# An LSTM layer on one core: a product of its own for f*c, other queues for some loads and stores, and more buffers

## Chip, cores and metric

The kernel runs on one core of a Trainium2 chip. The metric is the device time in microseconds (us) of one execution. The profile comes from one execution, recorded by the hardware profiler.

## What is computed

An LSTM over T=512 steps for a batch of 32, with D=H=512, all in fp32, whose input is added to its output. Cut to what matters:

```python
xW = einsum('ntd,dg->ntg', x, Wx) + b          # all steps at once
c = zeros
for t in range(512):
    a = xW[:, t] + h @ Wh                      # 32 x 2048
    i, f, o = sigmoid(a[:, :512]), sigmoid(a[:, 512:1024]), sigmoid(a[:, 1024:1536])
    g = tanh(a[:, 1536:])
    c = f * c + i * g
    h = o * tanh(c)
    y[:, t] = h
out = y + x
```

Only h @ Wh and the cell depend on the step before. The rest, xW, can be computed ahead.

## The kernel before, in words

**The recurrent part.** A state tile holds 128 partitions (4 blocks j of 32 batch rows, each for a quarter of the units) by 4 gates x 128 units. `h_part(t)` is 32 matmuls on PE, each 128x32 weights of h against a 128x512 slice of Wh (line L203), into one of two PSUM banks (`gbank`). That bank already holds the step's xW, put there by ACT (`seed_step`, L581). `cell(t)` then runs on ACT and VectorE (DVE): ACT does the sigmoid of i and f in one go (L217), tanh of g (L218), sigmoid of o (L219). VectorE makes i*g and f*c in one product of 128x256 (`prod`, L220), since c is kept beside g in the state tile `s`; then two adds of 64 units each (L222); ACT takes tanh of c in two halves (L224); VectorE multiplies by o (L226) and transposes (L232) into `ht`, which the next h_part needs. POOL adds x to it (L237), and SP stores two steps at a time (L241).

**The fill.** While the cell runs, PE computes xW for later steps. For 480 of the 512 steps it uses a fast matrix product in the manner of Strassen: steps are taken in 20 groups of 24. Each group has 20 slots; a slot has 7 products of sums of x by sums of Wx. The sums of x (U, `ubuf`) are made on VectorE (L381); the sums of weights are made once, at the start (L621), and stored in DRAM (`vdram`, six DMAs for a slot, L635); from there a ring of three SBUF rows, `vring`, is loaded in a fixed order (L544), one row of 896 KB for 7 products. The products (L470) go to `xbank` and `bbank`; ACT and VectorE move them to `cbuf` (L516, L522, L525, L526, L529, L532), VectorE sums them into results (L346), and SP stores results in DRAM (`xwd`, L362). Three steps ahead of its use, SP loads a step's xW from there into `xw` (`load_xw`, L568: four DMAs of 32 rows, 64 KB each). In a step, 46 or 48 matmuls of this fill ("passes", 128x256 each) stand behind h_part on PE.

**The head.** The first 24 steps' xW is made by plain products with the whole of Wx, in four chunks a step ("plain blocks", L164). The first five are made before step 0; after that most steps up to t=9 carry two plain blocks each. `keep` (L701) adds the bias to a finished block in one of two parks, which lie in `cbuf`, and SP stores it to `kept` in DRAM (L702). VectorE makes the weight sums meanwhile, and SP issues their stores (`flush_v`) after the next h_part. The stream of fast products begins at t=10. ACT's queue issues the loads of the bias (L709) and of two bias seeds (L676) at the very start; SP issues x, Wx, h0 and Wh.

**The tail.** The last 8 steps' xW is again plain, and the stream is over at about t=475. For this Wx is loaded once more (16 DMAs at t=477). From t=482 (`SPLIT`) each step is done in two halves: h_part in two halves of columns (64 matmuls), and a cell for each half, so that one half's cell runs beside the other half's matmuls. The two steps before SPLIT carry three plain chunks each, later ones carry one.

**What sets the order.** The instructions of each engine run in the order in which the program issues them (a manual schedule). In a step that is: h_part; on SP the stores of weight sums, of outputs and of kept blocks, the results' stores, the loads of x and xW; evacuation, seeds, vring loads, VectorE's sums as far as a planner's budget of time (`room`) reaches; the fill; the cell. Hardware DMAs issued by SP and by ACT share eight semaphores ("lanes") in turn, so a DMA is issued only when the one eight before it has landed.

Of the kernel before, what the change touches and what calls it, by code (L numbers as in the profile page):

```python
# [33 lines left out]
SPLIT = 482  # L34
# [54 lines left out]
def kernel(  # L89
# [22 lines left out]
    NC = 10  # L112
# [14 lines left out]
    h_init = const.tile([P, NJ, B], F32, name="h_init")  # L127
# [17 lines left out]
    late_weights = [False]  # L145

    def raw(blk):

        if late_weights[0] and blk < 6:
            return xs0[:, blk].rearrange("p s m -> p (s m)").rearrange("p (s c) -> p s c", s=4)  # L150
        return r1[:, blk]
# [16 lines left out]
    state = {"ht": h_init}  # L168
    sring = [work.tile([P, 2, 4, H], F32, name=f"s_{i}") for i in range(2)]
    oring = [work.tile([P, 2, H], F32, name=f"o_{i}") for i in range(1)]  # L170
    prod = work.tile([P, 2, 2, H], F32, name="prod")
    tanh_c = work.tile([P, P], F32, name="tanh_c")
    hbuf = work.tile([P, P], F32, name="hbuf")
    htr = [work.tile([P, NJ, B], F32, name=f"ht_{i}") for i in range(3)]
    ocr = [work.tile([P, 2, NJ, B], F32, name=f"oc_{i}") for i in range(2)]
    x_last = work.tile([P, P], F32, name="x_last")
# [30 lines left out]
    def cell(t):  # L207
# [3 lines left out]
        ht = htr[t % 3]  # L211
        by_gate = lambda a: a.rearrange("p (h g u) -> p h g u", g=G, u=H)
        for part in [(0,), (1,)] if is_split(t) else [(0, 1)]:
# [6 lines left out]
            nc.vector.tensor_mul(prod[:, i], s[:, i, 0:2], s[:, i, 2:4])  # L220
            for u in part:
                add(nxt[:, u, 3], prod[:, u, 0], prod[:, u, 1])  # L222
# [336 lines left out]
    def load_xw(t):  # L559
# [7 lines left out]
        for j in range(NJ):  # L567
            nc.sync.dma_start(  # L568
                out=dst[j * B : (j + 1) * B], in_=xwd[g % 2][m, q * B : (q + 1) * B, j]
            )  # L570
# [61 lines left out]
    def v_store(s, parts):  # L632
        lo, hi = parts
        to = lambda k: vdram[(s + k) % R]
        dma = lambda o, i: nc.sync.dma_start(out=o, in_=i)  # L635
        dma(to(0)[:, 0:2], lo[:, 0:2])
        dma(to(0)[:, 3], hi[:, 0])
        dma(to(1)[:, 2], lo[:, 2])
        dma(to(1)[:, 4], hi[:, 1])
# [9 lines left out]
    def v_slot(s):  # L649
# [4 lines left out]
        if len(terms) > 1:  # L654
            d = v_add(terms)
            v_stores.append(lambda: v_store(s, (vroom[d][:, 0:3], vroom[d][:, 3:7])))
            free_v.append(d)
        else:
            (i,) = terms
            parts = v_parts(i)  # L660
            v_stores.append(lambda: v_store(s, parts))
# [32 lines left out]
    parks = [cbuf[:, 8, 2 * i : 2 * i + 2].rearrange("p s c -> p (s c)") for i in range(2)]  # L694
# [3 lines left out]
    def keep(p):  # L698
        n = p - KEPT
        dst = parks[n % 2]  # L700
# [3 lines left out]
    with tc.manual_schedule():  # L704
# [3 lines left out]
        for j in range(NJ):  # L708
            nc.scalar.dma_start(  # L709
                out=bias_full[j * B : (j + 1) * B], in_=bias[j : j + 1].to_broadcast([B, W])  # L710
            )
        load_seeds(((4, 3), (5, 1)), nc.scalar)
        load_x(0, 0, 5)
        for c in range(4):
# [3 lines left out]
                in_=wx[c].rearrange("p (j c) -> p j c", j=NJ),  # L718
            )
# [7 lines left out]
        load_x(2)  # L727
        load_group(0)
# [28 lines left out]
        late_seeds_due = [late_seeds]  # L757
        s_done = {0: 4}
# [6 lines left out]
        for t in range(T):  # L765
# [17 lines left out]
            if t < HEAD_STEPS:  # L783
# [15 lines left out]
                for i, (kind, m) in enumerate(chunks):  # L799
                    if kind == "plain":  # L800
# [4 lines left out]
                        if i == 0:  # L805
                            cell(t)
# [7 lines left out]
                    else:  # L814
# [13 lines left out]
                        if i == 0:  # L828
                            cell(t)
# [107 lines left out]
```

## Time and profile before

| what | us |
| --- | --- |
| median of three runs | 3230.72 (3230.59 to 3233.8) |
| the profiled execution | 3234.63 |
| its span in the profile | 3232.8 |
| PE busy | 3163.2 (98% of the span) |
| VectorE busy | 2112.2 (65%) |
| ACT busy | 1342.8 (42%) |
| POOL busy | 233.9 (7%) |

The granted TensorE clock of the profiled execution was 0.992 of full speed in the mean. DMA engines moved 766.63 MB, 237 GB/s over the span.

By stages of the span (us), busy time of the engines, clock and DMA share:

| stretch | PE busy | VectorE busy | ACT busy | PE clock | DMA share |
| --- | --- | --- | --- | --- | --- |
| 60 to 80 | 19.01 | 8.70 | 1.85 | 1.00 | 0.69 |
| 80 to 100 | 12.41 | 8.69 | 1.61 | 0.91 | 0.79 |
| 100 to 120 | 8.78 | 10.70 | 1.61 | 0.74 | 0.62 |
| 120 to 140 | 16.25 | 11.62 | 2.49 | 0.91 | 0.78 |
| 140 to 160 | 18.59 | 10.01 | 3.21 | 1.00 | 0.49 |
| 160 to 180 | 10.20 | 4.17 | 2.52 | 0.74 | 0.75 |
| 180 to 200 | 18.64 | 12.46 | 7.42 | 1.00 | 0.73 |
| 200 to 240 | 38.37 | 31.22 | 17.84 | 1.00 | 0.81 |
| 240 to 280 | 34.35 | 28.00 | 14.66 | 0.96 | 0.69 |
| 400 to 3040 | 2638.35 | 1798.12 | 1154.19 | 1.00 | 0.77 |
| 3040 to 3100 | 48.13 | 23.62 | 16.73 | 0.91 | 0.61 |
| 3100 to 3200 | 100.00 | 45.29 | 47.75 | 1.00 | 0.24 |
| 3200 to 3232 | 25.95 | 15.43 | 13.47 | 0.99 | 0.06 |

How to read it: "busy" counts an engine's computing instructions, not the issue of DMAs. Matmuls are pipelined and their ends are modelled, so a PE that is busy for a whole stretch need not be at its peak. A wait is written as engine, tile and line of the waiting instruction, then "<-" and what released it, then the total in us, the number of times and the longest. In a timeline the bracket holds the idle time before the instruction and its releaser.

### The profile page before, as it was taken

Reading aid. Unit: us, or ns where it says so; the run is one execution under the profiler, and the core shown is the slowest. Engines: PE = TensorE matmul, PEld = TensorE weight load, DVE = VectorE, ACT = ScalarE, POOL = GpSimd, SP = SyncE. Lnnn points to the kernel's source line nnn. Section 1 sums busy time; section 2 is a strip of 40 time slices with the busy share of each in tenths; the row PEclk is TensorE's granted clock in tenths of the full one; section 3 lists DMA queues with packets and bytes.
Section 4 is the critical chain, followed back from the end, with each engine's and each line's share of the span. In section 5 each row is a group of like instructions: output and inputs, shape, how many; then the busy total and the mean of one; then the engine's idle time right before and its main releaser. Section 6 shows DMA issues by size and latency. Waiting matters only on the chain.

```text
span 3232.8 us, 102212 instructions
## 1 busy us (share of the span) xinstructions
PE 3163.2 (98%) x41304; PEld 1582.9 (49%) x41304; DVE 2112.2 (65%) x5721; ACT 1342.8 (42%) x4509; POOL 233.9 (7%) x508
## 2 busy tenths in 40 slices
PE   9789999999999999999999999999999999999999
PEld 4344545444444544444444544454444444444455
DVE  3566667676766667676666667676766767676634
ACT  0133444444444444444444444444444444444344
POOL 0000000000000000000000000000000000000000
PEclk9899999999999999999999999999999999999999
DMA  6677787877778777777777777877777777777641
GB/s 248 223 270 256 225 269 223 262 241 247 244 250 258 230 253 233 256 240 253 240 259 251 239 255 228 260 239 252 236 258 251 246 247 235 251 250 232 211 125 40
DMA packets 307080, 766.63 MB, mean 237 GB/s; under 512 B 49840, under 2 KB 95920, under 8 KB 306096
## 3 DMA queue, kind: packets, MB, share of 16 engines
q1 hardware_dynamic: 306128, 759.30, 73.1%
q8 instruction: 326, 5.34, 0.7%
q14 instruction: 146, 1.20, 0.1%
q10 hardware_dynamic: 480, 0.79, 0.1%
HBM read 577.18 MB, written 182.71 MB: 235 GB/s over the span
## 4 chain that ended last, share of the span: by engine, by line
PE 90%; DVE 1%; ACT 1%; issue 0%; DMA 0%; ACTq 0%; DVEq 0%
PE gbank L203 52%; PE xbank L470 31%; PE bbank L470 5%; PE xbank L203 2%; PE xbank L164 1%; DVE prod L220 0%; ACT s L217 0%; ACT tanh_c L224 0%; DVE ht L232 0%; DVE s L222 0%; DVE hbuf L226 0%; DMA xwd<-cbuf 0%; DVE cbuf L346 0%; ACT s L218 0%; DVE ubuf L381 0%
## 5 line engine op out<-in xcount | busy, mean ns | idle before, releaser
L203 PE MATMUL gbank<-wh_sb,ht 128*32 128x512 f32 (+1 forms) x16256 | 1809.1, 584 | 38.9 <-DVE ht L232 31.6
L470 PE MATMUL xbank<-vring,ubuf 128*32 128x256 f32 x14400 | 1110.6, 379 | 11.6 <-DMA vring<-vdram 9.8
L203 PEld LDWEIGHTS gbank<-wh_sb,ht 128*32 128x32 f32 x16256 | 577.8, 110 | 991.1 <-issue 755.9
L470 PEld LDWEIGHTS xbank<-vring,ubuf 128*32 128x32 f32 x14400 | 649.1, 110 | 378.7 <-issue 182.1
L220 DVE TENSOR_TENSOR prod<-s 128x256 f32<-128x256 f32 (+1 forms) x542 | 221.2, 408 | 853.6 <-ACT s L218 852.1
L217 ACT ACTIVATE s<-gbank 128x256 f32<-128x256 f32 (+1 forms) x509 | 192.1, 377 | 1376.8 <-PE gbank L203 1358.6
L346 DVE TENSOR_TENSOR cbuf<-cbuf 128x1024 f32<-128x1024 f32 x480 | 577.3, 1217 | 2.1
L237 POOL TENSOR_TENSOR oc<-xnat,ht 128x128 f32<-128x128 f32 x504 | 233.7, 464 | 2961.2 <-DVE ht L232 1478.9
L224 ACT ACTIVATE tanh_c<-s 128x64 f32<-128x64 f32 x1024 | 209.8, 249 | 387.5 <-DVE s L222 386.6
L581 ACT COPY gbank<-xw 128x512 f32<-128x512 f32 x477 | 285.0, 597 | 4.2 <-DMA xw<-xwd 4.0
L226 DVE TENSOR_TENSOR hbuf<-o,tanh_c 128x64 f32<-128x64 f32 x1024 | 192.8, 225 | 137.1 <-ACT tanh_c L224 137.0
L470 PE MATMUL bbank<-vring,ubuf 128*32 128x256 f32 x2400 | 277.0, 380 | 0.6 <-DVE cbuf L522 0.6
L516 ACT COPY cbuf<-xbank 128x512 f32<-128x512 f32 x400 | 231.6, 579 | 42.1 <-PE xbank L470 35.7
L470 PE MATMUL xbank<-vring,r 128*32 128x256 f32 x2400 | 239.0, 379 | 0.0
L470 PE MATMUL xbank<-vring,xs 128*32 128x256 f32 x2400 | 234.2, 381 | 1.0 <-ACT xbank L500 1.0
L222 DVE TENSOR_TENSOR s<-prod 128x64 f32<-128x64 f32 x1024 | 187.5, 222 | 18.6
L232 DVE STREAM_TRANSPOSE ht<-hbuf 128x64 f32<-128x64 f32 x1022 | 194.0, 225 | 6.6 <-DVE ht L232 0.4
L522 DVE TENSOR_TENSOR cbuf<-bbank,cbuf 128x256 f32<-128x256 f32 x400 | 162.9, 407 | 15.0 <-issue 12.6
L529 DVE TENSOR_TENSOR cbuf<-xbank,cbuf 128x256 f32<-128x256 f32 x400 | 161.9, 405 | 0.6 <-PE xbank L470 0.4
L526 DVE TENSOR_TENSOR cbuf<-xbank,cbuf 128x256 f32<-128x256 f32 x400 | 160.8, 402 | 1.7 <-ACT cbuf L525 1.7
L532 ACT COPY cbuf<-xbank 128x256 f32<-128x256 f32 x400 | 147.7, 369 | 19.8 <-PE xbank L470 3.1
L470 PEld LDWEIGHTS xbank<-vring,r 128*32 128x32 f32 x2400 | 122.8, 110 | 64.8 <-issue 38.1
(85 smaller groups left out, 1676.6 us busy)
## 6 DMA issues: line engine op xcount, KB each, us to landing
vring<-vdram SPq DMA_DIRECT2D x397, 896.0 KB, 6.3
xwd<-cbuf SPq DMA_DIRECT2D x240, 512.0 KB, 7.0
xw<-xwd SPq DMA_DIRECT2D x1920, 64.0 KB, 4.4
out_dram<-oc SPq DMA_DIRECT2D x255, 128.0 KB, 2.9
xnat<-in_x_dram SPq DMA_DIRECT2D x63, 512.0 KB, 5.0
xs<-in_x_grouped_dram SPq DMA_DIRECT2D x10, 1536.0 KB, 10.1
r<-in_x_grouped_dram SPq DMA_DIRECT2D x10, 1536.0 KB, 10.0
vdram<-vring SPq DMA_DIRECT2D x40, 128.0 KB, 1.9
```

The lines of the kernel that those rows point to most:

```text
L203: nc.tensor.matmul(dst[j * B : (j + 1) * B], state["ht"][:, k], m, start=False, stop=True, skip_group_check=True)
L217: nc.scalar.activation(s[:, i, 0:2], g[:, :, 0:2], AF.Sigmoid)
L220: nc.vector.tensor_mul(prod[:, i], s[:, i, 0:2], s[:, i, 2:4])
L222: add(nxt[:, u, 3], prod[:, u, 0], prod[:, u, 1])
L224: nc.scalar.activation(tanh_c[:, HALVES[u]], nxt[:, u, 3], AF.Tanh)
L226: nc.vector.tensor_mul(hbuf[:, HALVES[u]], o[:, u], tanh_c[:, HALVES[u]])
L232: nc.vector.transpose(ht[:, 2 * u : 2 * u + 2].rearrange("p q b -> p (q b)"), hbuf[:, HALVES[u]])
L237: (nc.gpsimd if t < T - 8 else nc.vector).tensor_add(oc[:, tt % 2], x_of(t), ht)
L346: op(c_of(dst), c_of(src), c_of(bb))
L470: nc.tensor.matmul(dst[q * B : (q + 1) * B], left_of(gr, s, r)[:, q * B : (q + 1) * B], vring[:, row % 3, RIGHT[r]], start=start, stop=Tru ...
L516: nc.scalar.copy(t[:, 0:4:3], xb.rearrange("p (n c) -> p n c", n=2))
L581: nc.scalar.copy(bank_of(t), src)
```

## The change

Six edits come together:

- **The cell.** `prod` is replaced by `fc` (f*c, 128x128, both halves at once) and `ig` (i*g, two products of 64 units). fc stands first, then the two i*g, then the two adds.
- **Stores of weight sums.** They are issued by ACT's queue in place of SP's, after the first cell of a step instead of after h_part; where a sum lies whole in one tile (14 of 20 slots), two of the six DMAs become one. The loads of the bias and of the early seeds go from ACT's queue to SP's, behind Wx and behind x; the late seeds are loaded by ACT's queue, one step after the last plain block, and made later.
- **Buffers.** Four parks instead of two, eleven `cbuf` buffers instead of ten; two `ht` buffers instead of three, and `h_init` and `x_last` lie in other buffers.
- **xW loads.** One DMA for a step, whose source pattern has the four blocks j as its outermost dimension, instead of four DMAs.
- **vring.** Its first rows may be loaded as soon as five or fewer jobs of VectorE are left and all stores of weight sums are issued, rather than at the first stream step.
- **Tail.** Wx is reloaded by six DMAs, one in each step from t=469; SPLIT is 478 instead of 482; the two steps before it carry two plain chunks instead of three.

```diff
@@ -31,7 +31,7 @@
 KEPT = 5
 AHEAD = 28
 STREAM0 = HEAD + GS - AHEAD
-SPLIT = 482
+SPLIT = 478
 U_SUMS = {6: {3: 1, 5: -1}, 7: {1: 1, 6: 1}, 8: {2: 1, 3: -1}, 9: {2: 1, 7: -1}, 10: {0: 1, 1: -1}, 11: {0: 1, 4: -1}}
 U_OF = [
@@ -109,7 +109,7 @@
     bbank = psum.tile([P, W], F32, name="bbank")
     gbank = [psum.tile([P, W], F32, name=f"gbank_{i}") for i in range(2)]
-    NC = 10
+    NC = 11
     r1 = const.tile([P, 8, 4, HW], F32, name="r1")
     cbuf = const.tile([P, NC, 4, HW], F32, name="cbuf")
     r2 = cbuf[:, 0:8]
@@ -124,7 +124,6 @@
     seeds = [r1[:, 6 + i // 2, i % 2 * 2 : i % 2 * 2 + 2].rearrange("p s c -> p (s c)") for i in range(4)]
     seeds += [seeds_own[:, i] for i in range(2)]
     bias_full = const.tile([P, W], F32, name="bias_full")
-    h_init = const.tile([P, NJ, B], F32, name="h_init")
     xw = const.tile([P, 3, W], F32, name="xw")
     vdram = dram.tile([R, P, 7, HW], F32, name="vdram")
@@ -143,12 +142,11 @@
         return xnat[:, xslot(t // TC), t % TC]
     late_weights = [False]
+    late_r = xs0.rearrange("p k s m -> p k (s m)").rearrange("p k (s c) -> p k s c", s=4)
     def raw(blk):
-        if late_weights[0] and blk < 6:
-            return xs0[:, blk].rearrange("p s m -> p (s m)").rearrange("p (s c) -> p s c", s=4)
-        return r1[:, blk]
+        return (late_r if late_weights[0] and blk < 6 else r1)[:, blk]
     def plain_block(t, c, bank):
@@ -165,15 +163,28 @@
                     d, x_of(t)[:, c], m, start=c == 0 and n == 0, stop=True, skip_group_check=True
                 )
-    state = {"ht": h_init}
+    def late_load(c, a, b):
+        rows = wx[c].rearrange("p (j s c) -> p j s c", j=NJ, s=2)
+        dst = late_r if a < 6 else r1
+        return lambda: nc.sync.dma_start(
+            out=dst[:, a:b, c % 2 * 2 : c % 2 * 2 + 2], in_=rows[:, a % 4 : a % 4 + b - a]
+        )
+
+    late_loads = [late_load(0, 0, 4), late_load(1, 0, 4), late_load(2, 4, 6), late_load(3, 4, 6)]
+    late_loads += [late_load(2, 6, 8), late_load(3, 6, 8)]
+
+    state = {}
     sring = [work.tile([P, 2, 4, H], F32, name=f"s_{i}") for i in range(2)]
     oring = [work.tile([P, 2, H], F32, name=f"o_{i}") for i in range(1)]
-    prod = work.tile([P, 2, 2, H], F32, name="prod")
+    fc = work.tile([P, 2, H], F32, name="fc")
+    ig = work.tile([P, 2, H], F32, name="ig")
     tanh_c = work.tile([P, P], F32, name="tanh_c")
     hbuf = work.tile([P, P], F32, name="hbuf")
-    htr = [work.tile([P, NJ, B], F32, name=f"ht_{i}") for i in range(3)]
+    htr = [work.tile([P, NJ, B], F32, name=f"ht_{i}") for i in range(2)]
     ocr = [work.tile([P, 2, NJ, B], F32, name=f"oc_{i}") for i in range(2)]
-    x_last = work.tile([P, P], F32, name="x_last")
+    x_last = vring[:, 0, 0, 0:P]
+    h_init = htr[1]
+    state["ht"] = h_init
     HALVES = [slice(0, H), slice(H, P)]
     PAIRS = [[xbank[0], xbank[1]], [gbank[0], gbank[1]]]
@@ -208,7 +219,7 @@
         n, tt = divmod(t, TC)
         s, nxt = sring[t % 2], sring[(t + 1) % 2]
         o = oring[0]
-        ht = htr[t % 3]
+        ht = htr[t % 2]
         by_gate = lambda a: a.rearrange("p (h g u) -> p h g u", g=G, u=H)
         for part in [(0,), (1,)] if is_split(t) else [(0, 1)]:
             i = slice(part[0], part[-1] + 1)
@@ -217,9 +228,11 @@
             nc.scalar.activation(s[:, i, 0:2], g[:, :, 0:2], AF.Sigmoid)
             nc.scalar.activation(s[:, i, 2], g[:, :, 3], AF.Tanh)
             nc.scalar.activation(o[:, i], g[:, :, 2], AF.Sigmoid)
-            nc.vector.tensor_mul(prod[:, i], s[:, i, 0:2], s[:, i, 2:4])
+            nc.vector.tensor_mul(fc[:, i], s[:, i, 1], s[:, i, 3])
             for u in part:
-                add(nxt[:, u, 3], prod[:, u, 0], prod[:, u, 1])
+                nc.vector.tensor_mul(ig[:, u], s[:, u, 0], s[:, u, 2])
+            for u in part:
+                add(nxt[:, u, 3], fc[:, u], ig[:, u])
             for u in part:
                 nc.scalar.activation(tanh_c[:, HALVES[u]], nxt[:, u, 3], AF.Tanh)
             for u in part:
@@ -564,10 +577,7 @@
         g, n = divmod(t - HEAD, GS)
         assert getattr(group(g), "stored", 0) >= 4 * (n // 8 + 1), (t, group(g).__dict__.get("stored"))
         m, q = divmod(n, 4)
-        for j in range(NJ):
-            nc.sync.dma_start(
-                out=dst[j * B : (j + 1) * B], in_=xwd[g % 2][m, q * B : (q + 1) * B, j]
-            )
+        nc.sync.dma_start(out=dst, in_=xwd[g % 2][m, q * B : (q + 1) * B].rearrange("b j c -> j b c"))
     xw_late = {}
@@ -629,14 +639,17 @@
             if v_uses[i] == 0:
                 free_v.append(vt[i])
-    def v_store(s, parts):
+    def v_store(s, parts, whole=None):
         lo, hi = parts
         to = lambda k: vdram[(s + k) % R]
-        dma = lambda o, i: nc.sync.dma_start(out=o, in_=i)
+        dma = lambda o, i: nc.scalar.dma_start(out=o, in_=i)
         dma(to(0)[:, 0:2], lo[:, 0:2])
         dma(to(0)[:, 3], hi[:, 0])
-        dma(to(1)[:, 2], lo[:, 2])
-        dma(to(1)[:, 4], hi[:, 1])
+        if whole is None:
+            dma(to(1)[:, 2], lo[:, 2])
+            dma(to(1)[:, 4], hi[:, 1])
+        else:
+            dma(to(1)[:, 2:5:2], whole[:, 2:5:2])
         dma(to(2)[:, 5], hi[:, 2])
         dma(to(3)[:, 6], hi[:, 3])
@@ -653,12 +666,12 @@
             v_sum(i)
         if len(terms) > 1:
             d = v_add(terms)
-            v_stores.append(lambda: v_store(s, (vroom[d][:, 0:3], vroom[d][:, 3:7])))
+            v_stores.append(lambda: v_store(s, (vroom[d][:, 0:3], vroom[d][:, 3:7]), vroom[d]))
             free_v.append(d)
         else:
             (i,) = terms
             parts = v_parts(i)
-            v_stores.append(lambda: v_store(s, parts))
+            v_stores.append(lambda: v_store(s, parts, vroom[vt[i]] if i > 7 else None))
             v_used(i)
     v_stores = []
@@ -691,13 +704,13 @@
-    parks = [cbuf[:, 8, 2 * i : 2 * i + 2].rearrange("p s c -> p (s c)") for i in range(2)]
+    parks = [cbuf[:, 8 + i // 2, i % 2 * 2 : i % 2 * 2 + 2].rearrange("p s c -> p (s c)") for i in range(4)]
     park_banks = [xbank[1], xbank[2], bbank]
     kept_stores = []
     def keep(p):
         n = p - KEPT
-        dst = parks[n % 2]
+        dst = parks[n % 4]
         add(dst, park_banks[n % 3], bias_full)
         kept_stores.append(lambda: nc.sync.dma_start(out=kept[n], in_=dst))
@@ -705,17 +718,16 @@
         nc.vector.memset(sring[0], 0.0)
         nc.vector.memset(tanh_c, 0.0)
         nc.scalar.activation(hbuf, tanh_c, AF.Sigmoid)
-        for j in range(NJ):
-            nc.scalar.dma_start(
-                out=bias_full[j * B : (j + 1) * B], in_=bias[j : j + 1].to_broadcast([B, W])
-            )
-        load_seeds(((4, 3), (5, 1)), nc.scalar)
         load_x(0, 0, 5)
         for c in range(4):
             ko, ki = divmod(c, 2)
             nc.sync.dma_start(
                 out=r1[:, 4 * ko : 4 * ko + 4, 2 * ki : 2 * ki + 2].rearrange("p j s c -> p j (s c)"),
                 in_=wx[c].rearrange("p (j c) -> p j c", j=NJ),
+            )
+        for j in range(NJ):
+            nc.sync.dma_start(
+                out=bias_full[j * B : (j + 1) * B], in_=bias[j : j + 1].to_broadcast([B, W])
             )
         nc.sync.dma_start(out=h_init.rearrange("p q b -> p (q b)"), in_=h0)
         for k in range(NJ):
@@ -725,6 +737,7 @@
         load_x(0, 5, 8)
         load_x(1)
         load_x(2)
+        load_seeds(((4, 3), (5, 1)), nc.sync)
         load_group(0)
         for n in range(3):
             for j in range(NJ):
@@ -755,6 +768,7 @@
         n_plain = 0
         group_loaded = 1
         late_seeds_due = [late_seeds]
+        plains_done = T
         s_done = {0: 4}
         v_ready = False
         plain_tail = []
@@ -764,7 +778,6 @@
         for t in range(T):
             h_part(t)
-            flush_v()
             for f in stores + kept_stores:
                 f()
             stores.clear()
@@ -804,9 +817,10 @@
                             plain_block(m, cc, bank)
                         if i == 0:
                             cell(t)
+                            flush_v()
                         keep(m)
-                        if n_plain == HEAD - KEPT and i == len(chunks) - 1 - sum(k == "stream" for k, _ in chunks):
-                            load_seeds(((0, 0), (1, 1), (2, 2)), nc.sync)
+                        if m == HEAD - 1:
+                            plains_done = t
                         while dve_jobs and room["dve"] > 0:
                             cost, f = dve_jobs.pop(0)
                             f()
@@ -816,7 +830,7 @@
                         u_ahead(m)
                         room["dve"] = m * PROD / 4 * 1.5
                         evacuate()
-                        if seeded[0] and late_seeds_due:
+                        if late_seeds_due and plains_done < t - 1:
                             late_seeds_due.pop()()
                         if t >= HEAD_STEPS - 3 and dve_jobs:
                             dve_jobs.pop(0)[1]()
@@ -827,10 +841,15 @@
                         emit_matmuls(m)
                         if i == 0:
                             cell(t)
+                            flush_v()
+                            if t == plains_done + 1:
+                                load_seeds(((0, 0), (1, 1), (2, 2)), nc.scalar)
                 if t + 1 >= KEPT:
                     seed_step(t + 1)
+                if len(dve_jobs) <= 5 and not v_stores:
+                    load_v_ahead()
                 if group_loaded == 1 and n_plain == HEAD - KEPT and not dve_jobs:
-                    flush_v()
+                    assert not v_stores
                     load_group(1)
                     group_loaded = 2
                     dve_jobs += [(cost_dve(768), lambda i=i: pair_sum(1, i)) for i in range(4)]
@@ -859,17 +878,13 @@
                 s_done[g] += 1
             while wqueue and room["dve"] > 300:
                 w_op()
-            if t == HEAD + NG * GS - 27:
+            if t == SPLIT - 9:
                 late_weights[0] = True
-                for blk in range(8):
-                    for ki in range(2):
-                        nc.sync.dma_start(
-                            out=raw(blk)[:, 2 * ki : 2 * ki + 2].rearrange("p s c -> p (s c)"),
-                            in_=wx[blk // 4 * 2 + ki].rearrange("p (j c) -> p j c", j=NJ)[:, blk % 4],
-                        )
+            if t >= SPLIT - 9 and late_loads:
+                late_loads.pop(0)()
             emit_matmuls(n)
             kept_late = []
-            for _ in range(0 if t < SPLIT - 2 else 3 if t < SPLIT else 1):
+            for _ in range(0 if t < SPLIT - 2 else 2 if t < SPLIT else 1):
                 if plain_tail:
                     p, c = plain_tail.pop(0)
                     plain_block(HEAD + NG * GS + p, c, tail_banks[p % 2])
```

## Prediction

> **What bounds the kernel now.** I read the page's chain of waits first, then the waits of PE and DVE in the long middle of the run (400 to 3040 us), then one step as the chain and as VectorE's timeline, then the head (0 to 290 us), and last the DMA queue.
>
> The page's chain is nearly all PE:
>
> ```profile
> PE 90%; DVE 1%; ACT 1%; issue 0%; DMA 0%; ACTq 0%; DVEq 0%
> PE gbank L203 52%; PE xbank L470 31%; PE bbank L470 5%; PE xbank L203 2%; PE xbank L164 1%; DVE prod L220 0%; ACT s L217 0%; ACT tanh_c L224 0%; DVE ht L232 0%; DVE s L222 0%; DVE hbuf L226 0%; DMA xwd<-cbuf 0%; DVE cbuf L346 0%; ACT s L218 0%; DVE ubuf L381 0%
> ```
>
> Read alone this says that only less matmul work can help. One step shows otherwise. This is the chain from 1600 to 1613 us (start, us, what), with the middle of each fill left out, and below it VectorE's part of the second cell:
>
> ```profile
> 1599.70 3.49 PE gbank L203 x32
> 1603.19 1.29 PE xbank L470 x24
> ...
> 1605.78 3.48 PE gbank L203 x32
> 1609.26 1.73 PE xbank L470 x32
> ...
> 1611.85 1.24 PE gbank L203 x9
> ```
> ```profile
> 1603.83 0.42 DVE L220 TENSOR_TENSOR prod<-s 128x256 f32<-128x256 f32 x1 [2.50 <-ACT s L218]
> 1604.29 0.36 DVE L222 TENSOR_TENSOR s<-prod 128x64 f32<-128x64 f32 x2
> 1604.90 0.37 DVE L226 TENSOR_TENSOR hbuf<-o,tanh_c 128x64 f32<-128x64 f32 x2 [0.25 <-ACT tanh_c L224]
> 1605.23 0.37 DVE L232 STREAM_TRANSPOSE ht<-hbuf 128x64 f32<-128x64 f32 x2
> ```
>
> The first fill counts 46 passes and the second 48, yet both steps are 6.07 us long. Of the 440 steps from t=30 to 469, 385 are about 6.07 and 55 are 6.02; the 55 are those where tanh L224 came 0.06 us earlier after its add. So the length of a step is set by the recurrent chain: h_part, sigmoid, tanh, product, add, tanh, product, transpose, next h_part. PE's matmul ends are modelled, and so its idle is hidden: in the records the next h_part starts 0.22 us after the start of the last fill pass (0.17 in the 6.02 us steps), where passes follow each other at 0.054. PE alone would allow about 6.07-0.22+0.054 = 5.90 us. That is the floor of any gain in the chain: 0.17 us a step.
>
> The head is bound otherwise. Waits of DVE and of PE from 0 to 290 us:
>
> ```profile
> DVE cbuf L701 <- DMA kept<-cbuf: 46.5, 6, 11.3
> ```
> ```profile
> PE gbank L203 <- DVE ht L232: 19.9, 5, 11.5
> PE xbank L470 <- DMA vring<-vdram: 9.8, 1, 9.8
> PE xbank L164 <- DVE cbuf L701: 5.0, 1, 5.0
> PE gbank L203 <- ACT gbank L581: 4.4, 1, 4.4
> PE gbank L164 <- DMA r<-in_L_cond_Wx_dram: 4.0, 1, 4.0
> ```
>
> VectorE, parking the plain blocks, waits for its two parks to be stored; the cell queued behind it is late, and PE waits for h. PE is busy 40.2 of the 60 us from 60 to 120, and after such a gap an h_part takes 5.3 us instead of 3.65 (granted clock 0.74 from 100 to 120).
>
> **Part by part**, against the profiled execution (3234.63 us; its span is 3232.8).
>
> *f*c apart.* From the end of h_part the sigmoid starts at +0.06 and takes 0.385, the candidate's tanh ends at +0.61, prod L220 (408 to 425 ns) starts at +0.64, and the first add at +1.10. VectorE waits for ACT ahead of prod in nearly every step (715.8 us in 417 waits), so it is free when the sigmoid ends. After: fc needs the sigmoid alone and starts at about +0.47. No row has a 128x128 product; between 128x64 (222 ns) and 128x256 (408) I take 285 ns. The first i*g (222 ns) then starts at +0.67, the second 0.14 later, and the add 40 ns after the first i*g, at +0.94. That is 0.15 earlier; I take 0.12, as VectorE gets one more instruction in the chain. Bounds: 0 and 0.17 (the floor above). Step 5.95; steps 10 to 474 are 465: **-55** (0 to -79).
>
> *Start.* PE's first plain block waits 4.0 us for Wx, landed behind bias and seeds, which share its DMA lanes. Wx now goes first, and four bias loads behind it on SP put Wh back by 4x0.45 = 1.8 us. That is hidden by PE's plain blocks, which keep it full from 20 to 40 us, and by VectorE's wait of 25.7 us ahead of its first bias add (L744), which already ends with Wh; if it weren't, it would take back the 1.8. **-2** (0 to -4).
>
> *Head.* Weight sums, 106 DMAs of some 0.45 us to issue (x6 took 2.87 us), leave SP for ACT, where each holds up what stands behind it: in steps 2 to 7, 10 to 21 of them follow the first cell and precede the next seed copy (L581), for which h_part waits. The block of 21 costs 10 us, of which the step's plain blocks (10.3 us of PE) hide nearly all. With four parks, and kept stores no longer behind weight sums on SP, the 46.5 us wait goes. Laying the steps out by hand, h_part(10) moves from 161.7 to 156.5. The stream's first pass waits 9.8 us more for vring today; the first rows now load before step 10, and I get a start at 160 instead of 175.2. I take **-12** (+5, if ACT's issues hold the cells as SP's now do, to -30, if they hold nothing).
>
> *Eleven result buffers.* The 4.4 us wait at 267 us is the seed copy behind L516, which waits 5.0 us for a result to be stored; another buffer should remove it: **-5** (0 to -6).
>
> *Tail.* From 3040 to 3100 PE is busy 48.1 of 60 us at a clock of 0.91: the stream ends at t=475 and unsplit steps run 6.1 to 8.7 us with little fill, one h_part waiting 2.5 us for a seed behind 16 weight loads. A split step with one plain chunk takes 4.47, and PE is full from 3100 to 3200. Four of six empty steps become split, the loads go one to a step (six in place of 16, about 0.45 us of SP each, into buffers last read some 15 steps before); but two more split steps at the end have no chunk. Of 12 idle and 5 us of slow clock I take **-10** (0 to -17).
>
> *Two htr buffers; x_last in vring.* The transpose of step t now overwrites h of step t-2. Its readers are h_part(t-1) and POOL's output sum L237 (464 ns), both a step done, so it costs 0; a POOL sum late by a whole step would add its lateness to the chain. x_last is written when the stream is over: 0.
>
> *One load per step.* SP saves three issues (about 0.45 each), and vring loads go out some 1.3 us earlier; today a vring row lands a median of 5.9 us ahead of use, in one phase of the group only 0.7. But the new source has four blocks outermost, where each of the old loads had 32 rows on both sides. Queue 1 and the loads, on the page:
>
> ```profile
> q1 hardware_dynamic: 306128, 759.30, 73.1%
> ...
> vring<-vdram SPq DMA_DIRECT2D x397, 896.0 KB, 6.3
> ...
> xw<-xwd SPq DMA_DIRECT2D x1920, 64.0 KB, 4.4
> ```
>
> No row shows such a transfer. If it spreads over 16 engines as today's do, it costs 0; I see no gain but the issues. If each block stays on one engine, four engines carry 65.5 KB of xw a step beside their share of the rest. From 400 to 3040 us queue 1 moved 643.4 MB in 76.4% of 16 engines: 50 us per MB and engine. A step moves 1.48 MB, 0.26 of it xw: 76+65.5 = 141.6 KB, or 7.1 us against a step of 6.07: +1.0 us a step, +480 in all. But that rate holds idle latency too: at the shortest packets in the trace (2 KB 84 ns, 7 KB 272 ns; mean of the latter 367) the same load is 5.6 to 5.7 us, under the step. So 0 to +480; I take 0, the shape's nearest row being today's four loads of the same bytes, and keep both ends.
>
> The Trainium skill speaks against this edit: DMA: Bandwidth & Descriptors, "Why a DMA increments its semaphore by 16 and not by 1", says that a DMA uses as many engines (at most 16) as divide the slowest dimension of both of its patterns, and the lowest-numbered ones. That would be four here, always the same; by it the price is the second case above, 5.6 to 7.1 us of four engines in each step. Every transfer of before has 16 by that rule, so no row tests it.
>
> Sum: -55-2-12-5-10 = -84; 3234.6 becomes 3150.6. The median of the runs is 3.9 lower, 3147. I predict **3150**.
>
> **Rivals.**
> *A, forecast (0.50)*: the one load is hidden; 3130 to 3195, by the terms' bounds.
> *B, it hides in part (0.13)*: vring rows come late in the phases with little margin, steps of 6.02 to 6.10: 3230.7-29+465x(-0.05 to +0.03) = 3178 to 3216.
> *C, it binds, slower (0.34)*: the four-block load delays the vring rows queued behind it on the same DMA engines, and PE waits for vring in the stream. Without the chain's term the rest is worth -29, so it decides from a step of 6.07+29/465 = 6.13. At 6.35 the time is 3332, at 7.1 3680. For it: DMA share 0.77 over the middle, and the arithmetic above. Against: the shortest packets fit.
> *D, ACT's stores hold back the cells (0.03)*: the head's -12 becomes +5 or worse, the rest stays: 3165 to 3175.
>
> Faster by over 0.2% (about what a measurement of this kernel tells from none): 0.50+0.12+0.03 less some slips, 0.60; the same 0.03; slower 0.37. The range leaves out C beyond a step of 6.45: 3130 to 3380; A's own is 3130 to 3195.
>
> **What would show it.** Chain: first add at about +0.95 after h_part, not +1.10, h_parts 5.95 apart. Load: no PE wait for vring between 400 and 3040 (0 today); if C, tens to hundreds of us there, and DMA engines unequally busy. Head: L701's successor waits under 10 us, first stream pass near 160. Tail: PE over 53 of 60 us in the same stretch. I am wrong if the fill ties PE first (steps stay near 6.05 with no wait) or the xw load binds.

## The result and the profile after

The changed kernel takes **3349.48 us** (median; 3344.65 to 3358.53) against 3232.26 for the kernel before on the same chip: a ratio of **1.036** (95% interval 1.034 to 1.039), slower by 117 us. The forecast of 3150 was wrong; the case it named C is what happened. The span of the profiled execution is 3351.7 us, 118.9 more than before's.

The start of each step's h_part in the two traces tells where the time went:

| stretch | before, us | after, us | difference |
| --- | --- | --- | --- |
| to h_part(0) | 30.3 | 25.4 | -5.0 |
| h_part(0) to h_part(10) | 131.4 | 142.7 | +11.4 |
| h_part(10) to h_part(23) | 137.5 | 122.3 | -15.2 |
| h_part(23) to h_part(473) | 2733.8 | 2858.8 | +125.0 |
| h_part(473) to the end | 199.8 | 202.5 | +2.7 |

So the loss is in the stream. Two groups of the page show it (line, engine, operation, tiles, count; then busy and mean ns; then idle before and its releaser), and the queues below them that bytes are not the reason:

```profile
L483 PE MATMUL xbank<-vring,ubuf 128*32 128x256 f32 x14400 | 1107.1, 384 | 100.2 <-DMA vring<-vdram 96.6
...
L591 ACT COPY gbank<-xw 128x512 f32<-128x512 f32 x473 | 282.2, 597 | 136.8 <-DMA xw<-xwd 94.3
```
```profile
q1 hardware_dynamic: 259936, 740.83, 67.0%
q10 hardware_dynamic: 17488, 19.14, 1.7%
```

The same two groups in the kernel before:

```profile
L470 PE MATMUL xbank<-vring,ubuf 128*32 128x256 f32 x14400 | 1110.6, 379 | 11.6 <-DMA vring<-vdram 9.8 <-DVE cbuf L526 1.4 <-ACT tanh_c L224 0.2
L581 ACT COPY gbank<-xw 128x512 f32<-128x512 f32 x477 | 285.0, 597 | 4.2 <-DMA xw<-xwd 4.0
```

PE now waits for vring 96.6 us (before 9.8, once, in the head), and ACT's seed copy waits 94.3 us for xw (before 4.0). Queue 1 was busy 73.1% before and is 67.0% now: the DMA engines are in the mean less loaded, and yet what they bring is late. From 400 to 3150 us alone, the waits of PE (total, times, longest) are led by

```profile
PE xbank L483 <- DMA vring<-vdram: 80.7, 28, 4.8
```

The stalls come in bursts. Of the steps between t=30 and 470 most are 5.93 to 6.05 us long, but 42 are over 7; they stand mostly in pairs 24 steps apart (t=29 and 30: 11.6 and 8.0; 53 and 54: 11.1 and 8.1; 77 and 78: 11.4 and 8.4), four or five steps after the load of a later group's x (one DMA of 1536 KB, once in 24 steps). The mean step is 6.35 us, before 6.08.

This is the stall of t=77: PE's timeline, and then the share of the 16 DMA engines and the rate in 40 slices of the 15 us from 630.

```profile
642.60 1.93 PE L483 MATMUL xbank<-vring,ubuf 128*32 128x256 f32 x16 [4.35 <-DMA vring<-vdram]
...
645.13 5.27 PE L214 MATMUL gbank<-wh_sb,ht 128*32 128x512 f32 x29
```
```profile
DMA  3955999999498999999722232322226526987999
GB/s 142 191 153 180 347 448 366 377 232 270 118 273 249 319 309 314 284 279 317 156 60 82 101 120 93 142 96 96 98 104 227 208 98 180 218 287 300 388 319 311
```

While PE waits, from 638.3 us on, the share is only 0.2 to 0.3 until 641.2: most engines have nothing to do. The packets that start there between 638 and 640 us are 56 of 2 KB (the size of the xW load's) and 13 of 7 KB (the size of a vring row's), mostly four in flight at a time. So the last packets of a vring row run on few engines, in turn with others.

A stall costs a second time. PE's busy time, granted clock and DMA share around it (stretch, length, PE, PEld, DVE, ACT, POOL, clock, share, GB/s):

```profile
638.00:644.00 6.00, 1.65 (x22) 0.83 (x17) 5.57 (x14) 1.40 (x7) 0.45 (x1) 0.80 0.47 161
644.00:650.00 6.00, 6.00 (x45) 1.86 (x41) 0.00 (x0) 1.08 (x2) 0.00 (x0) 0.63 0.64 232
```

The clock is 0.63 just behind the wait, and most of the h_part above takes 5.27 us in place of 3.64 for a whole one. From h_part(23) to h_part(473) PE waits 85.6 us for vring, and its h_parts are together some 40 us longer than without the one load (in e1 below); 19 of them take over 4.5 us, none there.

That one load a step uses few engines can be seen by itself in the late steps, where little else moves. This is the share of the 16 DMA engines and the rate, in 40 slices of the 10 us from 3224 in the kernel after, with two loads of 256 KB issued at 3224.4:

```profile
DMA  0106800322222222222222252222100000000005
GB/s 25 41 0 221 291 12 8 41 74 98 98 98 90 98 98 106 98 98 98 98 106 98 106 172 106 98 98 90 74 8 0 0 0 0 0 0 0 0 0 193
```

For 5 us the share is mostly 0.2 to 0.3 and the rate mostly 98 GB/s. A 2 KB packet takes 84 ns there (median), 24.4 GB/s; 98 GB/s are four engines without a pause. Each load takes about 2.7 us so, which is 32 packets of 84 ns.

### The profile page after: what moved, and what is told of

Read it like the earlier page. It is cut to its first block, busy times and chain, and to the rows that moved or that the text cites. A ratio compares the mean times of both kernels' runs of the same rounds, so it can differ in the third digit from the quotient of the medians.

```text
span 3351.7 us, 101512 instructions
## 1 busy us (share of the span) xinstructions
PE 3193.8 (95%) x41432; PEld 1856.8 (55%) x41432; DVE 2149.2 (64%) x6749; ACT 1350.9 (40%) x4525; POOL 233.0 (7%) x508
## 5 line engine op out<-in xcount | busy, mean ns | idle before, releaser
L214 PE MATMUL gbank<-wh_sb,ht 128*32 128x512 f32 (+1 forms) x16288 | 1872.6, 589 | 41.9 <-ACT gbank L591 34.0
L483 PE MATMUL xbank<-vring,ubuf 128*32 128x256 f32 x14400 | 1107.1, 384 | 100.2 <-DMA vring<-vdram 96.6
L214 PEld LDWEIGHTS gbank<-wh_sb,ht 128*32 128x32 f32 x16288 | 714.5, 111 | 879.1 <-issue 713.1
L483 PEld LDWEIGHTS xbank<-vring,ubuf 128*32 128x32 f32 x14400 | 712.3, 111 | 375.7 <-issue 238.9
L231 DVE TENSOR_TENSOR fc<-s 128x128 f32<-128x128 f32 (+1 forms) x546 | 153.5, 281 | 985.5 <-ACT s L228 984.6
L591 ACT COPY gbank<-xw 128x512 f32<-128x512 f32 x473 | 282.2, 597 | 136.8 <-DMA xw<-xwd 94.3
L483 PE MATMUL xbank<-vring,r 128*32 128x256 f32 x2400 | 221.4, 379 | 1.2 <-ACT tanh_c L237 1.2
L483 PE MATMUL xbank<-vring,xs 128*32 128x256 f32 x2400 | 217.4, 380 | 2.7 <-ACT xbank L513 1.0
L235 DVE TENSOR_TENSOR s<-fc,ig 128x64 f32<-128x64 f32 x1024 | 183.9, 218 | 2.3
L233 DVE TENSOR_TENSOR ig<-s 128x64 f32<-128x64 f32 x1024 | 183.5, 218 | 0.0
```

The source lines that it names most:

```text
L214: nc.tensor.matmul(dst[j * B : (j + 1) * B], state["ht"][:, k], m, start=False, stop=True, skip_group_check=True)
L233: nc.vector.tensor_mul(ig[:, u], s[:, u, 0], s[:, u, 2])
L235: add(nxt[:, u, 3], fc[:, u], ig[:, u])
L483: nc.tensor.matmul(dst[q * B : (q + 1) * B], left_of(gr, s, r)[:, q * B : (q + 1) * B], vring[:, row % 3, RIGHT[r]], start=start, stop=Tru ...
L591: nc.scalar.copy(bank_of(t), src)
```

## Experiments

The theory after the result: the one load, whose source has four blocks outermost, runs on four DMA engines, always the same, and what is queued behind it there (vring rows, group loads) lands late. The rivals: another part of the change makes the transfers late; or the load is slow because it is one large DMA. Beside it, two smaller questions: why the steps without a stall are 6.02 us and not 5.95, and why the head got no gain. All ratios are to runs of the kernel before on the same chip.

**e1, four loads again.**

```diff
-        nc.sync.dma_start(out=dst, in_=xwd[g % 2][m, q * B : (q + 1) * B].rearrange("b j c -> j b c"))
+        for j in range(NJ):
+            nc.sync.dma_start(
+                out=dst[j * B : (j + 1) * B], in_=xwd[g % 2][m, q * B : (q + 1) * B, j]
+            )
```

> The kernel after, with xw loaded by four DMAs of 32 rows again and nothing else changed. Theory (the one load with four blocks outermost loads a few DMA engines and delays the vring rows behind it): the vring waits of PE (79.7 us from 400 to 3100) and the xw waits of ACT's seed copy (85.3 us) go, steps are 5.95 to 6.02 throughout, and the time is 3160 to 3195 us. Rival 1 (the loss comes from the other edits, above all from fewer DMAs in the ring of lanes or from the changed order of SP): the waits stay and the time is above 3320. Rival 2 (the extra reads of Wx and vring rows in the stream take the DMA's time): half of it stays, 3240 to 3300.

Measured: 3193.85 us, ratio 0.988 (0.987 to 0.990). PE's waits for vring between 400 and 3020 us fall to 0.7 us, ACT's seed copy has no wait for xw there, h_part(23) to h_part(473) takes 2710.6 us, the mean step 6.02. The theory holds; both rivals of this run are out, since nothing else was changed back. The one load costs 156 us in this kernel.

**e2, the one load alone, in the kernel before** (the same edit the other way round).

> The kernel before with one xw load of 128 rows a step instead of four, and nothing else changed. Theory: step mean rises from 6.07 to about 6.35 as in the kernel after, in bursts after each group's load, +110 to +150 us: 3340 to 3380. If the loss needs another edit of the change with it (the earlier cell, the vring loads), it stays within 20 us of before.

Measured: 3367.97 us, ratio 1.043 (1.041 to 1.044). PE waits 76.2 us for vring in 26 waits from 400 to 3100 us, and the mean step of the same stretch (h_part(23) to h_part(473)) is 6.36. The load needs no other edit to cost 136 us.

**e3, two loads of two blocks.**

```diff
+        for j in (0, 2):
+            nc.sync.dma_start(
+                out=dst[j * B : (j + 2) * B],
+                in_=xwd[g % 2][m, q * B : (q + 1) * B, j : j + 2].rearrange("b j c -> j b c"),
+            )
```

> The kernel after with two xw loads a step, each with two blocks of 32 rows outermost. Theory with the number of outermost blocks as the number of engines: two engines carry 131 KB of xw beside 76 KB of the rest in a step, at the shortest packets (41 and 38 us per MB) 8.3 us: steps of 8.3 to 10, 4200 to 5000 us. Rival (a single big DMA is bad because of its size, or since one DMA waits where four overlapped): two are between one and four, 3170 to 3340.

Measured (two runs): 4506.84 us, ratio 1.394 (1.392 to 1.397): two loads are far worse than one. PE's waits from 400 to 4200 us (total, times, longest) begin

```profile
PE xbank L483 <- DMA vring<-vdram: 839.8, 210, 9.6
```

Share and rate in 40 slices of the 10 us from 1000 show it:

```profile
DMA  9733330011111011111101945955949999989979
GB/s 410 287 123 107 70 90 25 25 53 53 61 53 53 25 53 53 70 53 53 53 33 53 311 111 139 242 193 164 307 172 336 315 279 279 319 229 238 320 287 377
```

For 3.5 us the share is 0.1 and the rate mostly 53 GB/s, that of two engines. Half as many outermost blocks, half as many engines, and the same two for both loads of a step: on different pairs they would have spread over four, as one load does, and cost no more. By the expectation's sum 207 KB of a step pass through each of the two in its 8.84 us (an estimate). Two loads lie between one and four in size and number, and yet are slowest; that excludes size and number of the DMAs as the cause.

**e7, one load of 128 rows.** xwd is laid out so that a step's rows are consecutive; the results' stores are split in four for it.

```diff
-    xwd = [dram.tile([6, P, NJ, W], F32, name=f"xwd_{i}") for i in range(2)]
+    xwd = [dram.tile([6, 4, NJ, B, W], F32, name=f"xwd_{i}") for i in range(2)]
...
+        nc.sync.dma_start(out=dst, in_=xwd[g % 2][m, q].rearrange("j b c -> (j b) c"))
...
+            for q in range(4):
+                nc.sync.dma_start(
+                    out=xwd[gr.g % 2][2 * tau : 2 * tau + 2, q, j].rearrange("m b c -> b m c"),
+                    in_=cbuf[q * B : (q + 1) * B, buf].rearrange("p (m n) c -> p m (n c)", m=2),
+                )
```

> The kernel after with xwd laid out so that a step's xW is 128 consecutive rows: one load a step as in after, but its outermost dimension is 128 on both sides; each result is stored by four DMAs of 32 partitions in place of one. Theory (what costs is the four outermost blocks, which keep a load on four DMA engines, not that the load is one DMA of 256 KB): the waits for vring and xw go, 3180 to 3205. Rival (one DMA of this size in place of four delays what is behind it): above 3300.

Measured: 3186.15 us, ratio 0.986 (0.984 to 0.988). From 400 to 3000 us PE has no wait for vring. One DMA of 256 KB a step is as good as four, if its outermost dimension is 128. The same late stretch of this kernel, 10 us from 3056:

```profile
DMA  0095954999960000003000000000000000000086
GB/s 0 20 311 193 82 82 188 360 361 352 418 230 25 0 0 0 0 0 66 0 0 0 0 0 0 0 0 0 0 0 0 0 0 0 0 0 0 0 307 217
```

Loads of the same bytes now take a share of 0.9 and run at 350 to 418 GB/s, in place of 0.2 at 98, and are done in about a microsecond each.

**e4, f*c apart, in the kernel before.**

```diff
...
-            nc.vector.tensor_mul(prod[:, i], s[:, i, 0:2], s[:, i, 2:4])
+            nc.vector.tensor_mul(fc[:, i], s[:, i, 1], s[:, i, 3])
             for u in part:
-                add(nxt[:, u, 3], prod[:, u, 0], prod[:, u, 1])
+                nc.vector.tensor_mul(ig[:, u], s[:, u, 0], s[:, u, 2])
+            for u in part:
+                add(nxt[:, u, 3], fc[:, u], ig[:, u])
```

> The kernel before with f*c as its own product, and nothing else changed. Theory: the add starts 0.14 us earlier after h_part and the step falls from 6.07 to between 5.95 and 6.02: 3176 to 3210. Rival (another thing than the chain holds h_part, since unstalled steps of the kernel after are still 5.99 to 6.05): less than 15 us gained, above 3215.

Measured: 3205.78 us, ratio 0.992 (0.990 to 0.993). From the end of an h_part to the next one it is now 2.29 us where it was 2.43: the chain became 0.14 us shorter, as reckoned. But the mean step went from 6.08 only to 6.02. Something other than the chain now sets most steps; e9 and e10 were made to find it.

**e9 and e10, a seventh of the fill left out**, in e1 and in the kernel before: the products r = 6, which only add into a bank. The output lacks them.

```diff
-            nc.tensor.matmul(
+            if r != 6:
+                nc.tensor.matmul(
...
```

> e1 without one of the seven products of each slot (r = 6, which only adds into a bank): a sixth to a seventh of the fill's matmuls is left out, the plan of the steps is unchanged; the output lacks these products. Theory (with fc apart, PE itself bounds a step: 8 groups of h_part at 428 ns and 12 groups of fill at 216 ns are 6.02 us, whether the last group is whole or not, and the chain is shorter): most steps fall from 6.02 to the chain's length, 5.92 to 5.97; 20 to 45 us less than e1, 3150 to 3175. Rival (another wait than PE's work holds the step at 6.02): it stays at 6.00 or more and the time within 10 us of e1.

> The kernel before without the same product of each slot; the output lacks it. Theory (before, the chain bounds the step): steps stay 6.07, the time within 6 us of before. Rival (PE bounds before too): steps fall by 0.1 or more, below 3195.

Measured, one run each: e9 3157.29 us, 36.6 below e1; e10 3229.18, 4.6 below the median of before. In e10 the mean step is 6.07, as good as unchanged: before, the fill was hidden and the chain set the step. In e9 351 of 440 steps are under 5.93 (29 in e1): with fc apart, the fill sets the step, and with less of it the chain shows. It can be read off the chain of e9 (start, us, what), one step:

```profile
1585.26 3.67 PE gbank L214 x32
1588.93 0.02 issue
1588.95 0.39 ACT s L228
1589.35 0.02 issue
1589.37 0.29 DVE fc L231
1589.66 0.27 DVE ig L233 x2
1589.93 0.15 DVE s L235
...
1590.16 0.27 ACT tanh_c L237
1590.43 0.02 issue
1590.45 0.29 DVE hbuf L239 x2
...
1591.16 0.01 issue
1591.17 1.88 PE gbank L214 x13
```

5.91 us, and every piece is h_part or a link of the cell. Against it a step of the kernel after without a stall, PE's timeline (start, us, line, tiles, count):

```profile
455.58 3.64 PE L214 MATMUL gbank<-wh_sb,ht 128*32 128x512 f32 x32
459.01 0.64 PE L483 MATMUL xbank<-vring,ubuf 128*32 128x256 f32 x8
459.44 0.64 PE L483 MATMUL bbank<-vring,ubuf 128*32 128x256 f32 x8
459.87 1.07 PE L483 MATMUL xbank<-vring,ubuf 128*32 128x256 f32 x16
460.74 0.64 PE L483 MATMUL xbank<-vring,xs 128*32 128x256 f32 x8
461.17 0.64 PE L483 MATMUL xbank<-vring,ubuf 128*32 128x256 f32 x8
461.60 3.64 PE L214 MATMUL gbank<-wh_sb,ht 128*32 128x512 f32 x32
```

Eight passes take 0.43 us, h_part 3.43, no gap: 3.43 + 6x0.43 = 6.02. Steps with 46 passes are hardly quicker: in e1 they take 6.00 us in the mean (nine in ten between 5.92 and 6.03), those with 48 take 6.04. The single records suggest why. Passes start in groups of four (34, 7 and 7 ns apart, then 168 to the next group in before), 216 ns a group of the fill and 428 ns a group of h_part; 8 groups of h_part and 12 of fill are 6.02 us, and 46 passes are eleven and a half groups. That a broken group costs nearly a whole one is argued from this and not shown by a run.

**e5, stores of weight sums on SP again; e6, the seed copy ahead of ACT's stores; e12, e5 with two parks.** e5 is e1 with the first of these edits, e6 is e1 with the second (made at both of the cell's places), e12 is e5 with the third:

```diff
-        dma = lambda o, i: nc.scalar.dma_start(out=o, in_=i)
+        dma = lambda o, i: nc.sync.dma_start(out=o, in_=i)
```
```diff
...
                             cell(t)
+                            if t + 1 >= KEPT:
+                                seed_step(t + 1)
                             flush_v()
...
-                if t + 1 >= KEPT:
-                    seed_step(t + 1)
```
```diff
-        dst = parks[n % 4]
+        dst = parks[n % 2]
```

> e1 (the kernel after with four xw loads) with the stores of weight sums issued by SP again, at the same place in the program (after the step's first cell); nothing else changed. Theory (issue on ACT holds the seed copy, for which h_part waits 35.4 us in four waits of e1, and undoes what the parks gain): h_part(10) starts at 150 to 162 us instead of 168.6, the seed waits go, 3175 to 3188. Rival (kept stores behind weight sums on SP hold the parks again, as in before): h_part(10) no earlier than 168 and 3194 or more.

> e1 with the seed copy for the next step issued before the flush of weight-sum stores on ACT, right behind the first cell; nothing else changed. Theory: the copy no longer stands behind the 5 to 14 us of issues, h_part(10) starts 5 to 15 us earlier than in e1 (153 to 163), 3179 to 3189. Rival (the next cell then waits for the same issues): h_part(10) within 3 us of 168.6 and 3191 to 3197.

> e5 with two parks instead of four, nothing else changed. Theory (the parks end the head's stall): VectorE waits for stored parks again, 20 us or more, and h_part(10) is 15 to 30 us later than in e5, 3175 to 3190. Rival (it was the flush behind the cell instead of behind h_part, and the fewer stores): h_part(10) within 5 us of e5's 127.4, 3158 to 3166.

| kernel | us (median) | ratio (interval) | h_part(10) at | PE's or VectorE's wait |
| --- | --- | --- | --- | --- |
| e1 | 3193.85 | 0.988 (0.987 to 0.990) | 168.6 | h_part for ACT's seed copy 35.4 |
| e5 | 3160.25 | 0.977 (0.976 to 0.979) | 127.4 | VectorE for stored parks 9.8 |
| e6 | 3171.45 | 0.981 (0.979 to 0.982) | 142.9 | h_part for the transpose 13.5 |
| e12 | 3156.8 | 0.978 (0.975 to 0.980) | 133.5 | VectorE for stored parks 26.3, h_part for the transpose 3.1 |

The issue on ACT is what eats the head's gain: it costs 34 us between e1 and e5, more than e5's theory had (3175 to 3188, h_part(10) at 150 to 162). ACT's timeline in e1 shows the block (21 DMAs here) between the cell's last tanh and the seed copy, for which the next h_part waits; the bracket is the idle time before the copy and what ended it:

```profile
79.88 0.33 ACTq L648 DMA_DIRECT2D vdram<-ubuf  x1
79.88 0.24 ACT L237 ACTIVATE tanh_c<-s 128x64 f32<-128x64 f32 x1
80.24 5.09 ACTq L648 DMA_DIRECT2D vdram<-ubuf  x9
85.38 0.46 ACTq L648 DMA_DIRECT2D vdram<-r  x1
85.88 0.46 ACTq L648 DMA_DIRECT2D vdram<-cbuf  x1
86.38 0.46 ACTq L648 DMA_DIRECT2D vdram<-r  x1
86.88 1.48 ACTq L648 DMA_DIRECT2D vdram<-cbuf  x3
88.40 2.85 ACTq L648 DMA_DIRECT2D vdram<-vring  x5
91.29 0.59 ACT L594 COPY gbank<-xw 128x512 f32<-128x512 f32 x1 [11.18 <-DMA vdram<-vring]
```

PE in 20 us stretches from 60 to 120 (stretch, length, busy PE, PEld, DVE, ACT, POOL, clock, DMA share, GB/s), first of e1, then of e5:

```profile
60.00:80.00 20.00, 17.42 (x228) 10.37 (x223) 10.22 (x23) 2.13 (x10) 0.46 (x1) 1.00 0.89 300
80.00:100.00 20.00, 8.07 (x74) 3.06 (x78) 11.42 (x23) 1.83 (x7) 0.48 (x2) 0.66 0.66 227
100.00:120.00 20.00, 8.99 (x80) 3.02 (x76) 6.11 (x14) 1.72 (x6) 0.42 (x1) 0.74 0.63 213
```
```profile
60.00:80.00 20.00, 20.00 (x256) 11.77 (x250) 17.02 (x34) 2.73 (x11) 0.91 (x2) 1.00 0.89 307
80.00:100.00 20.00, 19.33 (x232) 10.22 (x228) 16.19 (x33) 3.22 (x12) 0.92 (x2) 1.00 0.93 318
100.00:120.00 20.00, 20.00 (x256) 12.09 (x255) 9.83 (x28) 3.28 (x12) 0.91 (x2) 1.00 1.00 337
```

In e1 PE is busy less than half of the time from 80 to 120, and its clock falls to 0.66; in e5 it is nearly full at 1.00. e6 gets 26 of the 41 us at h_part(10): that is more than its theory allowed (5 to 15 us), and its rival (no gain) falls too. The rest stays lost, since the copy goes ahead but the next cell still stands behind the issues. **A theory that fell** is that of e12: two parks bring VectorE's wait back to 26.3 us, but cost 6 us at h_part(10), made good by h_part(11), and nothing in the whole (3156.8 against 3160.25, whose intervals overlap). Its rival had 5 us and 3158 to 3166, and is missed by little. So the number of parks was not what ended before's stall. What is left is above all the flush right after the cell instead of behind the next h_part, with fewer stores; that was not tried by itself, and the cause of this gain stays open.

**e8, the tail as before, in e1.**

```diff
-SPLIT = 478
+SPLIT = 482
...
-            if t == SPLIT - 9:
+            if t == HEAD + NG * GS - 27:
                 late_weights[0] = True
-            if t >= SPLIT - 9 and late_loads:
-                late_loads.pop(0)()
+                while late_loads:
+                    late_loads.pop(0)()
```

> e1 with the tail as before: SPLIT 482, all reloads of Wx at t=477 (still as six DMAs), three plain chunks in the two steps before SPLIT. By the prediction's sum the tail edit is worth 10 us: 3204. From the stages of e1 against the kernel with f*c alone (from h_part(473) to the end 193.9 against 197.4 us) it is worth 3 to 5: 3197 to 3200. Rival (spreading the reloads into the stream costs more than it gives, since PE waits 3.6 us for vring there): 3190 or less.

Measured: 3201.53 us, ratio 0.990 (0.989 to 0.992), 7.7 us above e1. The tail edit is worth 6 to 8 us; from h_part(473) to the end e8 takes 200.3 us and e1 193.9. In e1 step 475 still takes 11.9 us, with 3.6 us of PE's waits for vring: six reloads of Wx now move beside the stream's last vring rows. In e8 that step takes 8.6 us with no such wait, and in e7, which has these reloads but one load of 128 rows a step, 8.7.

**e11, 128-row loads and stores on SP** (e7 with e5's edit).

> e7 (one load of 128 rows, results stored by four DMAs) with the stores of weight sums issued by SP as in e5. Theory (the two losses add up): e5's head with e7's stream, 3150 to 3165. If the 128-row load was only worth something beside stores on ACT, it is at or above e5's 3160.

Measured: **3152.02 us** (3151.3 to 3154.0), ratio **0.975** (0.973 to 0.976), the fastest here. h_part(10) starts at 126.1 us and the mean step is 6.01. Its rival (at or above e5's 3160) falls: against four loads, the 128-row load saves some 8 us of the median beside stores on SP (e5) as beside stores on ACT (e7 against e1). The two cures add up.

## Why the prediction was wrong

- **One load per step: the step that failed.** Of the bounds 0 and +480 us the prediction took 0, "the shape's nearest row being today's four loads of the same bytes". That row says nothing of the shape: it has 32 rows outermost, not four blocks. Measured +156 (e1 against after) and +136 (e2). The arithmetic for four engines was right: 141.6 KB a step at the 6.35 us it came to is 45 us per MB and engine, between the shortest packets (5.6 to 5.7 us) and the stretch's mean (7.1). (84 ns is the median of before's 2 KB packets rather than the shortest, 81; this changes little.) Rival C had the mechanism, place and order of size (3332 at a step of 6.35), and the range held 3349 only because it took in a part of C. What was mis-judged is the weight of the lower end: it had 0.3 us to spare in an even flow, but x comes in one load of 1.5 MB a group. That is 96 KB for each of 16 engines, some 4 us at 41 us per MB (an estimate from 2 KB packets of 84 ns), and four engines that are already nearly full fall behind with it. The stalls stand a few steps after these loads, 24 steps apart. What the sum did not have at all is the clock behind each stall. The rule of the Trainium skill that the prediction set beside it (DMA: Bandwidth & Descriptors, "Why a DMA increments its semaphore by 16 and not by 1": the largest number of engines, at most 16, that divides the slowest dimension of both sides, and the lowest-numbered ones) agrees with what was measured: 98 GB/s at four blocks, 350 to 418 GB/s at 128 rows, 53 GB/s at two blocks. Which engines they were no run shows.
- **f*c apart: right in the chain, wrong in the floor.** The add was to come at +0.94 after h_part; it came at +0.95 to 0.96, and the chain shrank by 0.14 (reckoned 0.12 to 0.15). The gain was -26 us (e4's stretch from h_part(23) to h_part(473): 2708.0 against 2733.8), not -55. The term that failed is "PE alone would allow about 5.90 us": it took the 0.17 to 0.22 us ahead of h_part for idle time, since passes follow each other at a mean pitch of 0.054. But they start in groups of four, and 168 ns stand ahead of every group: most of that was no idle time of PE. With fc apart, h_part and twelve groups of fill are 6.02 us. The prediction named this among the things that would prove it wrong ("the fill ties PE first"), with 6.05.
- **Head: no gain for the edit as made.** -12 was forecast from ACT's issues being hidden by plain blocks; h_part(0) to h_part(10) got 11 us longer. At the first stream pass, to which the forecast reckoned (160 in place of 175.2), the kernel after is at 171.5: 3.7 earlier, with 5 from the start, so the head's term is about +1. 10 us for a block of 21 was close (11.2), but the seed copy waits for the whole block in four steps, and PE is then idle and its clock low. Rival D was this mechanism, at 0.03 and with +5 or worse. The gain was there to be had: e5 reaches h_part(11) 38 us ahead of the kernel before, 5 of it from the start, which is a little more than the -30 allowed.
- **Start** -5 (forecast -2). **From h_part(10) to (23)** -15: the vring wait of 9.8 us (counted in the head's term) and the seed wait of 4.4 are gone, as forecast; the edits behind them were not tried one by one. **Tail** -6 to -8 with four loads a step (forecast -10); in the kernel after, the late vring rows turned it into +2.7.

With four loads again, e1 shows the rest of the sum: its profiled execution is 37 us shorter than before's, not 84. Of the 47 missing, the chain's term makes some 32 (-23 in e1 and -26 in e4 against -55), start, head and buffers together 11 (-8 at h_part(23) against -19), the tail 4 (-6 against -10).

## What to carry to other kernels

Before merging DMAs, look at the outermost dimension of both sides: here the same 256 KB ran at 98 GB/s with four blocks outermost and at over 350 GB/s with 128 rows, and the mean DMA share even fell while transfers came late. When a chain is shortened, work out the next floor in the units in which the engine really takes its work (here, as the records suggest, groups of four passes), not from a mean pitch. And DMAs issued from an engine in the recurrence hold up everything behind them there: a block of 21 took 11 us of ACT, and moving these stores to SP was worth 34 us.

## What was not expected of the hardware

Two blocks outermost are much worse than four (4507 against 3349 us), though each DMA is half the size: fewer engines and not smaller DMAs are what counts. And idle time of PE costs a second time here: a PE full of matmuls kept a clock of 1.00 in e5's head, while a PE busy for 8 to 9 of 20 us had 0.66 to 0.74. So h_part(5), (6) and (8) took 5.6 to 6.3 us in e1 and 3.6 to 3.7 in e5, and 19 h_parts behind the stalls of the stream took 4.6 to 6.1 us.
